# Scores before maxima in the second burst of an attention step

## The chip, the cores and the metric

The kernel runs on one core of one Trainium2 chip. The metric is device time in microseconds (us) of one execution. Before the change it was 2928.36 us, the median of 3 runs (2923.62 to 2931.43).

## The reference, cut to what matters

The input `x` has 4 sequences of 2048 tokens with 256 channels. Four blocks follow each other, each added to its input: an attention with one head of 64 (called `a` or `a0` here), a linear layer whose input is rounded to fp8, an attention with 16 heads of 16 (called `a1`), and a gated layer that mixes each token with the one before it. The change lies in the 16-head attention:

```python
Q, K, V = (proj(W_Q), proj(W_K), proj(W_V))          # 16 heads of 16
Q = _apply_rope(Q, cos, sin)
K = _apply_rope(K, cos, sin)
scores = jnp.einsum('bhsd,bhtd->bhst', Q, K) / jnp.sqrt(jnp.float32(D_K))
scores = jnp.where(causal[None, None], scores, -jnp.inf)
attn = jax.nn.softmax(scores, axis=-1)
out = jnp.einsum('bhst,bhtd->bhsd', attn, V)
```

Everything else is other work for this text: projections, transposes, the first attention, the two layers, the residual sums.

## The kernel before, in words

**Tiling.** Tokens are cut into 16 blocks of 512 (4 sequences `b`, 4 blocks `qb` in each). In the 16-head attention the heads go in 4 groups `g` of 4. A step is one `(b, qb, g, kt)`: 128 keys `kt` against the 512 queries of a block, for four heads `h` at once. A group has `4 * (qb + 1)` steps, and the program 640.

**Three shapes of the TensorE array.** A head has 16 channels, kept as a high and a low part side by side, so 32 rows are enough. The matmuls of `maxima_of` and `scores_of` therefore use tiles of 32 rows by 128 columns: head `h` uses the row group `h`, and four heads can run side by side. `weighted` (L860) multiplies the softmax weights by the values, with 128 rows by 32 columns. All other matmuls use the whole array. The text calls these three the row shape, the column shape and the full shape.

**What a step computes.** The softmax needs the maximum of each query before its exponentials. So a step does two things for two different groups:
- `scores_of(..., h)` for the present group: a matmul that adds the negated maximum (`sh`, the shift, in bfloat16, with the weights `ones`), one with the high part of the queries (`qh`) and one with the low part (`ql`), both float32r; on the diagonal two bfloat16 mask matmuls (L817) more. ScalarE then takes the exponential (`p`, L824). In the first step of a group the shift comes last.
- `maxima_of(..., h)` for the next group: a matmul with `qh` and one with `ql` (L779), both float32r, on the diagonal two mask matmuls (L788) more. VectorE then takes the maximum over the keys (`mx`, L794).

The text writes `m` for the output tile of a maximum and `s` for that of a score; each is one PSUM bank. The seven banks are shared by everything except the accumulator of `weighted`.

**The order of a step.** The kernel writes its own order out, and an order is kept on each engine by dependencies that are added at the end. A step issues

1. the first burst (L1211): scores of heads 0 and 1, maxima of heads 2 and 3,
2. `weighted` of the step before (L1217),
3. the second burst (L1229): maxima of heads 0 and 1, scores of heads 2 and 3,
4. `pull` (L1239): other work, if the planner finds it due.

`together` (L833) interleaves the four row groups of a burst: it goes round the rows and takes one matmul from each. A row that has not begun is held back while the planner counts no free bank (`room`, L827). In the first burst, a row that is through may start the scores of heads 2 and 3 early (`spare`, L853).

**The planner.** `Clock` (L41) follows each emitted instruction with assumed costs. It gives out the bank that comes free first, and `pull`, `rate_of` and `force` decide by its times in which step a piece of other work is put. In one line of it (L178) the first matmul of a row group after a change of shape is late by an amount that goes by its type and width:

```python
late = 0 if kind.endswith("float16") else 15 if mode[1] == SLOT else 45 if n <= P else 90
```

Of the kernel before, what the change touches and what calls it, by code (L numbers as in the profile page):

```python
# [30 lines left out]
HG = 4  # L31
# [159 lines left out]
def seq_kernel(  # L191
# [71 lines left out]
    order = [(b, qb) for b in range(B) for qb in range(NB)]  # L263
# [100 lines left out]
    def avbank(name):  # L364
        return pav.tile([P, BLK], F32, tag="av", name=name)

    def w2(name, dtype=F32):
        live[0] += 1
        return work.tile([P, BLK], dtype, tag="w2", name=name, bufs=W2)
# [7 lines left out]
    def done(n):  # L377
        live[0] -= n
# [418 lines left out]
    def scores_of(b, qb, g, kt, sh, pTs, h):  # L797

        r = slice(h * SLOT, (h + 1) * SLOT)
        c0 = max(kt - qb * TT, 0) * P  # L800
        keys = kT1[b, kt // TT][r, g, (kt % TT) * P : (kt % TT + 1) * P]
        diag = kt >= qb * TT
        sc = bank(f"s_{b}_{qb}_{g}_{kt}_{h}")

        q = q1[b, qb, g // 2]
        todo = [(keys, z[r, g % 2, c0:]) for z in q]
        todo.insert(0 if kt else 2, (ones[r, :], sh[r, c0:]))
        for i, (lhsT, rhs) in enumerate(todo):
            nc.tensor.matmul(  # L809
                sc[:, c0:], lhsT, rhs, start=(i == 0), stop=(i == 2 and not diag)  # L810
            )
            if i < 2 or diag:
                yield
        if diag:
            for v in range(2):
                hi = (v + 1) * P // 2
                nc.tensor.matmul(  # L817
                    sc[:, c0 : c0 + hi], mask_k[r, v, :], mask_q[r, v, :hi],
                    start=False, stop=(v == 1),
                )  # L820
                if v < 1:
                    yield
        pTs[h] = work.tile([P, BLK], F32, tag="pT", name=f"p_{b}_{qb}_{g}_{kt}_{h}", bufs=PT)
        nc.scalar.activation(pTs[h][:, c0:], sc[:, c0:], AF.Exp, scale=DK**-0.5)  # L824
        yield

    def room(h):  # L827

        clock.follow()
        now = max(clock.issue, clock.rows[h]) + 50  # L830
        return sum(b not in clock.held and t <= now for b, t in clock.banks.items())

    def together(rows, spare=()):  # L833

        rows = [[[part, False] for part in r] for r in rows]
        spare = dict(spare)
        wait = True
        while any(rows):  # L840
            moved = False
            for h, r in enumerate(rows):
                while r:
                    if wait and not r[0][1] and not room(h):
                        break
                    try:
                        next(r[0][0])
                        r[0][1] = moved = True
                        wait = True
                        break  # L850
                    except StopIteration:
                        r.pop(0)
                if not r and h in spare and any(rows) and room(h) > 3:  # L853
                    next(spare.pop(h))
            wait = moved
# [11 lines left out]
    def to_tokens(g, cs, cn, tag):  # L867

        pt = bank(f"pt_{tag}")
        for t in range(TT):  # L870
            nc.tensor.transpose(pt[:, t * P : (t + 1) * P], cs[:, t * P : (t + 1) * P], ident)  # L871
        nat = pt.rearrange("p (t h s) -> p t h s", t=TT, h=HG)
        rs = small.tile([P, TT, HG], F32, tag="rs1", name=f"rs_{tag}")
        nc.vector.reciprocal(rs, nat[:, :, :, DK])
        nc.vector.tensor_tensor(
            cn[:, :, g * HG * DK : (g + 1) * HG * DK].rearrange("p t (h d) -> p t h d", h=HG),
            nat[:, :, :, :DK],
            rs[:, :, :, None].to_broadcast([P, TT, HG, DK]),
            ALU.mult,
        )  # L880
# [133 lines left out]
    def b_of(i):  # L1014
        b, qb = order[i]
        x = xs[b, qb]
        b_load[0], q_load[0] = 14.0, 1.0
        Bq.extend([b_queries(b, qb, 0, 0), b_queries(b, qb, 0, 1), b_keys(b, qb),
                   b_project(b, qb), b_in(b, qb, x, 0), b_in(b, qb, x, 1)])
        Q.extend(b_queries(b, qb, 1, hf) for hf in range(2))  # L1020

    def end_of(i, cn):
        b, qb = order[i]
        x = xs[b, qb]
        e_load[0] = 17.0
        E.extend(end_half(b, qb, x, cn, hf) for hf in range(2))

    def begun(i):
        return all((*order[i], "cT", hf) in flags for hf in range(2))
# [66 lines left out]
    def refill(i):  # L1096

        nonlocal a_next
        if not A and a_next < min(i + (4 if not E and at[1] > 0 else 3), N):
            a_load[0] = 0.0  # L1100
            A.extend(a_of(a_next))
            a_next += 1
# [19 lines left out]
    def rate_of(i, g, kt, n):  # L1122

        to = lambda where: max(where * n - (g * n + kt), 1)
        spare = sum(loads[id(z)][0] for z in (A, Bq, Q, E)) + sum(
            a_work(*order[j]) for j in range(a_next, min(i + 4, N))
        )
        rate = min(BASE, spare / to(4))
        first = a_load[0] if a_next == i + 2 else 0.0
        if first > 0 or Bq:  # L1130
            rate = max(rate, first / to(1.5), (first + b_load[0] + e_load[0] / 2) / to(3))
        return max(rate, (q_load[0] + e_load[0]) / to(4))
# [30 lines left out]
    def due_maxima(position):  # L1163

        nonlocal b_done
        out = []
        while ahead and ahead[0][0] <= position + 1e-6:
            if ahead[0][1] > b_done:
                force(Bq)
                b_done = ahead[0][1]  # L1170
            out.append(ahead.pop()[2:])
            z = next(mq, None)
            if z:
                ahead.append(z)
        return out
# [14 lines left out]
    for G, (i, b, qb, g) in enumerate(groups):  # L1190
        n = steps[G]
        at[:] = i, g, 0, n
        if g == 0 and i + 1 < N:
            b_of(i + 1)
        av = avbank(f"av_{b}_{qb}_{g}")
        for kt in range(n):
            at[2] = kt
            count[0] += 1
            if i > 0 and (g, kt) == (0, 2):
                end_of(i - 1, cns.pop(i - 1))  # L1200
            refill(i)
            rate = rate_of(i, g, kt, n)
            credit = min(credit + rate, rate + 1.5)
            first = A if a_next == i + 2 else None
            mine = [Bq, E, Q] if i == 0 or begun(i - 1) else [E, Bq, Q]
            lists = [first] + mine if first else mine + [A]
            ms = due_maxima(G + kt / n)
            pTs, c0 = {}, max(kt - qb * TT, 0) * P
            S = [scores_of(b, qb, g, kt, shifts[G], pTs, h) for h in range(HG)]
            M = [[maxima_of(*ms[0][0], h)] if ms else [] for h in range(HG)]  # L1210
            together([[S[0]], [S[1]], M[2], M[3]], {h: S[h] for h in (2, 3) if kt})  # L1211
            if tail is not None:
                to_tokens(*tail)
                done(1)
                tail = None
            if last is not None:
                weighted(*last)  # L1217
                clock.follow()
                if narrow and clock.when(*narrow[0][4]) < clock.pe + SLACK:
                    narrow_values()  # L1220
                if last[2] != g:
                    cs = w2(f"cs_{G - 1}")
                    nc.scalar.copy(cs, last[4])
                    if g == 1:
                        while i > 0 and not begun(i - 1):
                            assert pull_first([E])
                        cns[i] = work.tile([P, TT, C], F32, tag="cn", name=f"cn_{b}_{qb}", bufs=1)
                    tail = (last[2], cs, cns[i] if g > 0 else cns[i - 1], f"c_{G - 1}")
            together([M[0], M[1], [S[2]], [S[3]]])  # L1229
            last = (b, qb, g, kt, av, pTs, c0)  # L1230
            if ms:
                ms[0][1]()
            clock.follow()
            for m in ms[1:]:
                whole_maxima(m)
            if kt == n - 1 and G + 1 < len(groups):
                shift_of(G + 1)
                clock.follow()
            pull(lists, 0.0)  # L1239
        if g == NG - 1:  # L1240
            force(E)
            force(Q)
# [84 lines left out]
```

## Time and profile before

| what | value |
|---|---|
| median of 3 runs | 2928.36 us (2923.62 to 2931.43) |
| the profiled execution's own time | 2922.84 us |
| its span, from the first to the last instruction | 2921.0 us |
| mean granted TensorE clock | 0.979 |
| TensorE (PE) busy | 2804.3 us, 96% |
| VectorE (DVE) busy | 2012.6 us, 69% |
| ScalarE (ACT) busy | 1688.2 us, 58% |
| GpSimd (POOL) busy | 1011.8 us, 35% |

A busy time is the union of the instructions' times on that engine. Matmuls are pipelined and run side by side in the row shape, so a busy TensorE is not one at its peak, and a matmul that stands in the array behind another one of its row group counts as busy. `PEld` is TensorE's loading of weights. Lines such as L779 are lines of the kernel.

### The profile page before, as it was taken

To read this page: it belongs to the slowest core of one execution; us is meant where nothing else is said; L and a number is where in the kernel's file an instruction comes from. 1 tells how busy PE (TensorE), PEld (TensorE's weight loads), DVE (VectorE), ACT (ScalarE), POOL (GpSimd) and SP (SyncE) were. 2 spreads that over 40 slices of the span, in tenths; PEclk is the share of its full clock that TensorE was granted. 3 is DMA by queue.
4 is the path that set the end of the run, shared out by engine and by line. 5 is a ranking of instruction groups with operands and counts; after the bars stand their busy time and mean duration, and the time that the engine had idled before them with its cause. 6 is when DMAs were issued, how large, how long until landed. Compare 5 with 4: busy or idle time off the path is not lost.

```text
span 2921.0 us, 68258 instructions
## 1 busy us (share of the span) xinstructions
PE 2804.3 (96%) x27616; PEld 1580.6 (54%) x27616; DVE 2012.6 (69%) x4279; ACT 1688.2 (58%) x3553; POOL 1011.8 (35%) x1534
## 2 busy tenths in 40 slices
PE   6899999999999999999999999999999999999997
PEld 3555555555456555555556555555545655555443
DVE  4567667787556786787746777778764677678761
ACT  2456555566665556656665555656566565665663
POOL 4534425242333514514215342523323342450001
PEclk8799999999999999999999999999999999999999
DMA  3000000000000000000000000000000000000000
GB/s 91 1 12 5 12 12 16 12 2 26 2 12 16 5 23 2 16 12 5 23 12 5 12 5 23 5 23 1 27 2 12 16 5 16 1 9 1 5 1 12
DMA packets 28781, 36.70 MB, mean 13 GB/s; under 512 B 3312, under 2 KB 22064, under 8 KB 28464
## 3 DMA queue, kind: packets, MB, share of 16 engines
q1 hardware_dynamic: 28464, 32.32, 3.9%
q8 instruction: 217, 3.56, 0.5%
q14 instruction: 100, 0.82, 0.1%
HBM read 11.24 MB, written 8.39 MB: 7 GB/s over the span
## 4 chain that ended last, share of the span: by engine, by line
PE 79%; DVE 11%; POOL 5%; issue 3%; ACT 1%; DMA 0%; SPq 0%; POOLq 0%; ACTq 0%; DVEq 0%
PE av L860 18%; PE s L809 16%; PE m L779 14%; DVE mx L794 7%; PE pq_a L421 3%; PE pv_a L421 2%; PE av_a L578 2%; PE m_a L524 2%; PE po_f L421 2%; PE pk_f L928 2%; PE pw_f L421 2%; PE pr_f L421 2%; PE m L788 1%; PE s_a L548 1%; PE pt_c L871 1%
## 5 line engine op out<-in xcount | busy, mean ns | idle before, releaser
L794 DVE TENSOR_REDUCE mx<-m 128x1 f32<-128x512 f32 (+3 forms) x2560 | 1405.1, 603 | 531.6 <-PE m L779 237.6
L824 ACT ACTIVATE p<-s 128x512 f32<-128x512 f32 (+3 forms) x2560 | 1214.2, 534 | 814.3 <-PE s L809 445.8
L779 PE MATMUL m<-kT_a,qh_a 32*128 32x512 f32 (+3 forms) x2560 | 686.1, 458 | 13.7 <-ACT p L824 4.0
L809 PE MATMUL s<-qh_a,kT_a 32*128 32x512 f32 (+3 forms) x2560 | 672.6, 508 | 0.5 <-ACT p L824 0.5
L860 PE MATMUL av<-p,v_a 128*32 128x512 f32 (+3 forms) x5120 | 641.0, 545 | 0.1
L779 PEld LDWEIGHTS m<-kT_a,qh_a 32*128 32x128 f32 x2560 | 296.0, 184 | 493.9 <-issue 161.1
L779 PE MATMUL m<-kT_a,ql_a 32*128 32x512 f32 (+3 forms) x2560 | 559.3, 368 | 0.0
L809 PE MATMUL s<-ql_a,kT_a 32*128 32x512 f32 (+3 forms) x2560 | 494.3, 365 | 0.0
L809 PE MATMUL s<-sh,ones 32*128 32x512 bf16 (+3 forms) x2560 | 481.0, 355 | 3.1 <-DVE mx L794 2.3
L779 PEld LDWEIGHTS m<-kT_a,ql_a 32*128 32x128 f32 x2560 | 297.0, 188 | 3.3 <-issue 1.0
L809 PEld LDWEIGHTS s<-qh_a,kT_a 32*128 32x128 f32 x2560 | 259.7, 189 | 35.3 <-issue 23.7
L809 PEld LDWEIGHTS s<-ql_a,kT_a 32*128 32x128 f32 x2560 | 257.3, 187 | 2.8 <-issue 0.2
L809 PEld LDWEIGHTS <-ones 32*128 32x128 bf16 x2560 | 128.7, 91 | 171.4 <-issue 150.5
L860 PEld LDWEIGHTS av<-p,v_a 128*32 128x32 f32 x5120 | 112.4, 108 | 161.8 <-issue 118.7
L443 POOL CAST pad<-nm 128x16 bf16<-128x16 f32 x64 | 17.0, 266 | 380.9 <-DVE nm L989 352.3
L590 POOL TENSOR_TENSOR sum_a<-sum_a,p_a 128x512 f32<-128x512 f32 (+1 forms) x128 | 146.3, 1143 | 5.0
L788 PE MATMUL m<-mask_k,mask_q 32*128 32x64 bf16 x2048 | 147.0, 196 | 0.0
L817 PE MATMUL s<-mask_q,mask_k 32*128 32x64 bf16 (+1 forms) x2048 | 140.4, 207 | 0.0
L590 POOL TENSOR_TENSOR cx_a<-cx_a,avs_a 128x512 f32<-128x512 f32 (+1 forms) x64 | 73.1, 1143 | 155.1 <-ACT avs_a L588 155.1
L421 PE MATMUL pq_a<-wqkv,xT_a 128*128 128x512 f32 x256 | 122.8, 602 | 1.6 <-DVE mx L794 1.3
L950 POOL TENSOR_TENSOR x<-x,sg_f 128x512 f32<-128x512 f32 x32 | 41.4, 1294 | 177.3 <-DVE sg_f L949 177.1
L935 POOL TENSOR_TENSOR ka_f<-ka_f 128x512 f32<-128x512 f32 x32 | 33.2, 1038 | 186.1 <-ACT ka_f L934 186.1
(164 smaller groups left out, 4015.6 us busy)
## 6 DMA issues: line engine op xcount, KB each, us to landing
x<-in_x SPq DMA_DIRECT2D x16, 512.0 KB, 4.0
out_y<-x SPq DMA_DIRECT2D x32, 256.0 KB, 2.1
qh_a<-th_a SPq DMA_DIRECT2D x32, 128.0 KB, 2.3
ql_a<-tl_a SPq DMA_DIRECT2D x32, 128.0 KB, 2.3
kT_a<-th_a SPq DMA_DIRECT2D x16, 128.0 KB, 2.3
kT_a<-tl_a SPq DMA_DIRECT2D x16, 128.0 KB, 2.3
wqkv<-in_wqkv1T SPq DMA_DIRECT2D x1, 768.0 KB, 7.3
wc<-in_wfT SPq DMA_DIRECT2D x1, 256.0 KB, 5.7
```

The source lines that it names most:

```text
L421: nc.tensor.matmul(dst, lhsT[:, k, t * P : (t + 1) * P], w[:, k, :], start=(k == 0), stop=(k == CK - 1),)
L524: nc.tensor.matmul(sc[:, :w], q[:, t * P : (t + 1) * P], kT0[kb][:, :w], start=(q is qh), stop=(kb < qb and q is ql),)
L578: nc.tensor.matmul(av[z * SLOT : (z + 1) * SLOT, c0:], v0[kt // TT][:, kt % TT + j, d * SLOT : (d + 1) * SLOT], pTs[j][:, c0:], start=True ...
L590: nc.gpsimd.tensor_tensor(to[:, c0:], to[:, c0:], add[:, c0:], ALU.add)
L779: nc.tensor.matmul(sc[:, :w], q1[b, qb, g // 2][i][r, g % 2, t * P : (t + 1) * P], kT1[b, kb][r, g, :w], start=(i == 0), stop=(kb < qb and ...
L788: nc.tensor.matmul(sc[:, w - P + lo : w - P // 2 + lo], mask_q[r, v, :], mask_k[r, v, lo : lo + P // 2], start=False, stop=(v == 1),)
L794: nc.vector.reduce_max(mx[:, t, h, kb : kb + 1], sc[:, :w], axis=AX.X)
L809: nc.tensor.matmul(sc[:, c0:], lhsT, rhs, start=(i == 0), stop=(i == 2 and not diag))
L817: nc.tensor.matmul(sc[:, c0 : c0 + hi], mask_k[r, v, :], mask_q[r, v, :hi], start=False, stop=(v == 1),)
L824: nc.scalar.activation(pTs[h][:, c0:], sc[:, c0:], AF.Exp, scale=DK**-0.5)
L860: nc.tensor.matmul(av[h * SLOT : (h + 1) * SLOT, c0:], v1[b, kt // TT][:, kt % TT, at : at + SLOT], pTs[h][:, c0:], start=(kt == 0), stop= ...
L928: nc.tensor.matmul(pk[:, d * HALF : (d + 1) * HALF], wk[:, k, d * P : (d + 1) * P], xk[:, k, :], start=(k == 0), stop=(k == CK - 1),)
```

## The change

The second burst goes round its rows in the order 2, 3, 0, 1 in place of 0, 1, 2, 3. Rows 2 and 3 hold the scores of heads 2 and 3, rows 0 and 1 the maxima of heads 0 and 1. The first burst and all other callers keep the order 0, 1, 2, 3. No instruction is added or removed.

```diff
-    def together(rows, spare=()):
+    def together(rows, spare=(), order=range(HG)):
...
-            for h, r in enumerate(rows):
+            for h in order:
+                r = rows[h]
                 while r:
                     if wait and not r[0][1] and not room(h):
                         break
...
-            together([M[0], M[1], [S[2]], [S[3]]])
+            together([M[0], M[1], [S[2]], [S[3]]], order=(2, 3, 0, 1))
```

## The prediction

> **What bounds the kernel now.** I read the page first: the span, the engines' busy times and the chain that ended last.
>
> ```profile
> span 2921.0 us, 68258 instructions
> PE 2804.3 (96%) x27616; PEld 1580.6 (54%) x27616; DVE 2012.6 (69%) x4279; ACT 1688.2 (58%) x3553; POOL 1011.8 (35%) x1534
> PE 79%; DVE 11%; POOL 5%; issue 3%; ACT 1%; DMA 0%; SPq 0%; POOLq 0%; ACTq 0%; DVEq 0%
> PE av L860 18%; PE s L809 16%; PE m L779 14%; DVE mx L794 7%; PE pq_a L421 3%; PE pv_a L421 2%; PE av_a L578 2%; PE m_a L524 2%; PE po_f L421 2%; PE pk_f L928 2%; PE pw_f L421 2%; PE pr_f L421 2%; PE m L788 1%; PE s_a L548 1%; PE pt_c L871 1%
> ```
>
> TensorE sets the time, and the three groups that the change moves around lead the chain. But 7% of it (some 200 us) is VectorE's maximum, so there are places where TensorE waits for a bank. Next, the timeline of one second burst, behind `weighted` and ahead of other work:
>
> ```profile
> 2705.62 0.61 PE L860 MATMUL av<-p,v_a 128*32 128x512 f32 x4
> 2706.16 0.50 PE L779 MATMUL m<-kT_a,qh_a 32*128 32x512 f32 x2
> 2706.17 0.39 PE L809 MATMUL s<-sh,ones 32*128 32x512 bf16 x2
> 2706.21 0.58 PE L809 MATMUL s<-qh_a,kT_a 32*128 32x512 f32 x2
> 2706.49 0.40 PE L779 MATMUL m<-kT_a,ql_a 32*128 32x512 f32 x2
> 2706.62 0.40 PE L809 MATMUL s<-ql_a,kT_a 32*128 32x512 f32 x2
> 2706.92 1.29 DVE L794 TENSOR_REDUCE mx<-m 128x1 f32<-128x512 f32 x2 [0.68 <-PE m L779]
> ```
>
> All four rows start within 0.02 us. A maximum's second matmul comes 0.33 us behind its first; the scores' third comes 0.46 us behind the shift, and ends the burst. Now a first burst that begins with the shift after another shape, which is the order that the change gives to the second burst:
>
> ```profile
> 242.61 0.39 PE L809 MATMUL s<-sh,ones 32*128 32x512 bf16 x2
> 242.62 0.50 PE L779 MATMUL m<-kT_a,qh_a 32*128 32x512 f32 x2
> 242.65 0.58 PE L809 MATMUL s<-qh_a,kT_a 32*128 32x512 f32 x2
> 242.96 0.39 PE L779 MATMUL m<-kT_a,ql_a 32*128 32x512 f32 x2
> 243.07 0.40 PE L809 MATMUL s<-ql_a,kT_a 32*128 32x512 f32 x2
> ```
>
> The same distances: 0.34 us for the maximum, 0.46 us for the scores. Last, the chain of waits in a stretch of steps with no other work between the bursts:
>
> ```profile
> 2689.57 1.01 PE av L860 x8
> 2690.57 0.33 PE m L779
> 2690.90 0.24 PE s L809 x3
> 2691.14 0.14 PE m L779 x2
> 2691.28 0.69 DVE mx L794
> 2691.97 0.04 issue
> 2692.01 0.73 PE m L779 x2
> ```
>
> Such a step is bare: its second burst and the next step's first burst want eight banks, there are seven, and the eighth tile waits until VectorE has taken the first maximum.
>
> **The change part by part.** I read TensorE's matmul records one by one against the order of the built program, before and after.
>
> *What moves.* 488 second bursts began with two maxima and two shifts behind a column-shape matmul; now 483 begin with shifts. 57 bursts that hold scores alone do not change. No DMA moves, no engine gets an instruction more, and ScalarE's and VectorE's own order within a burst stays.
>
> *The start after the change of shape.* Second bursts begin 70 ns ahead of the modelled end of the last matmul when a maximum leads (425 records), 67 ns when a shift leads (57). So a shift in front costs 3 ns. Stalls there are absent: 9 of 10 lie within 1 ns of that.
>
> *The loading of weights.* The groups by line give 184 ns for a maximum's weights and 91 ns for the shift's. Were the load exposed, 93 ns in 483 bursts would be 45 us gained; the 70 against 67 ns say that it is hidden, and I take nothing. The Trainium skill ("TensorE: Matmul & The Clock Gate", section "LDWEIGHTS (loading the stationary operand)") has a load's time depend on its columns alone, which would make the two equal and the gain zero as well; the rows differ by half, and only the start times settle it.
>
> *The dear first matmul.* At 512 columns a float32r matmul takes 213 ns when it follows another in its row group, and 336 ns when it is the first there after a change of shape. That is 120 ns for rows 0 and 1 in every second burst, 59 us in all, if a shift in front of the burst paid it for all rows. In 188 second bursts with a maximum in front the distance is 336 ns; in 58 first bursts behind L421 with the shift in front, 337. The price belongs to each row group, and the change leaves each row its own first matmul. Value: nothing.
>
> *The order of issue.* In 302 first bursts the rows start at 0, 3, 4 and 7 ns (shift, shift, maximum, maximum); in second bursts now at 0, 3, 9 and 13 (maxima, shifts). With the 3 ns above, scores come 6 ns earlier and maxima 7 ns later. Where a burst of the same make-up stands alone between other shapes, its length can be compared: 715 ns shift first (117 bursts) against 726 ns maximum first (114) at 512 columns, 647 against 661 with scores of 384, but 673 against 667 with scores of 256, where the maximum's row is the longer. Some 280 lone bursts at -10 ns, 75 at +6 and some 190 bare ones at +7 (the maximum's bank ends their loop): -2.8 + 0.5 + 1.3 = -1.0 us. Bounds: -11 and +7 ns on all, -6 to +4 us. The Trainium skill (same page, "Part 3: Packing small matmuls — row/col tiling", "The mechanism") has matmuls start strictly in program order. By that rule the scores' `qh`, which is issued behind the maximum's `ql`, could not start before it, and the new order would free it 0.28 us earlier, over 100 us for 483 bursts. The burst at 2706 shows `qh` at 2706.21 and `ql` at 2706.49: the rows run on their own, and I go by the row.
>
> *Rows that the planner holds back.* Where it counts fewer than four free banks, the last row of the round begins late. Before, that was a score in 35 bursts; after, a maximum in 39, and in 13 of these both maxima (52 tiles). A lone burst with a late row took 1102 against 726 ns when it was a score, and 941 against 715 when the first burst's last row was late: 39 x 0.226 - 35 x 0.376 = -4 us. But 34 of the 52 tiles (11 first and 23 second maxima) stand in bare steps, where a late maximum can hold the loop, up to 34 x 0.376 = +13 us. I take +1, nearer to the first, since the first of the two maxima, whose bank ends the loop, is late in only 11.
>
> *The other work.* This is where most of the change lies. The planner's times move by some ns, and it decides anew: of 1248 pieces of other work on TensorE, 624 land in another step, most within five steps. Their number is the same, but stretches of row-shape matmuls fall from 1097 to 1084, and 13 fewer stretches of full-shape work begin. I price each kind by its mean time in the trace, from the end of the matmul before to the start of the one behind. Stretches with one step's share of maxima and scores: 23 fewer at 0.796 us, -18.3. Stretches of two bursts: 12 more at 2.09, +25.2. Two more of four bursts with other work behind at 3.62, +7.2; two fewer with three pairs of maxima at 2.14, -4.3; three fewer with scores in both and maxima in one at 1.13, -3.4; the rest (scores alone) +1.5. Sum +7.9 us. Joining two stretches of other work saves 0.07 us of the change of shape and some 0.06 to 0.11 us of a first matmul: 13 x 0.15 = -2. That leaves +6 us. A bare step hides less than two covered ones, so fewer interruptions do not pay. The spread of such stretches around their mean is some 0.3 us, half of them change, and three of the four sequences repeat one pattern, so that errors add up: I take +-9 us.
>
> **Sum.** -1 + 1 + 6 = +6 us on the profiled execution's 2922.84, that is 2928.8. The median of the runs lies 5.5 us above that execution; carried over, 2928.4 + 6 = 2934.4, which I call 2934. A measurement of this kernel tells about 0.3%, 9 us, from no change.
>
> **The rivals.**
>
> *Slower: late maxima in the bare loop.* Place: the bare steps, some 190 stretches. Mechanism: a maximum's bank is freed only when its last matmul is through and VectorE has taken 0.69 us over it; behind two scores in the issue order it may come through when they do. VectorE already waits for scores to release it (the list of waits has 141 us, 147 times, on L809). Price: the scores' last matmul ends 0.14 us behind the maximum's in the burst at 2706 (2706.62 + 0.40 against 2706.49 + 0.39); 190 x 0.14 = +27 us, with the +6 some 2961. It decides once the second matmul of full maxima stands behind the scores' last in the program. In the built order that is so for 13 first maxima and 39 second ones, and for none before; of the remaining full ones none. So it acts in a tenth of the places unless late rows delay their successors too. A mild form, +15 us in all, is the likelier.
>
> *Faster: less switching.* 26 fewer changes of shape and scores that reach ScalarE earlier. If the new places of the other work happen to fill bare steps that are dearer than the mean (two bursts and more cost 2.1 to 3.6 us), ten such at 0.9 us of stall (2.09 less five matmuls of 213 ns in a row group and 120 for the first) and the 2 us of switching give -11, some 2917.
>
> *Faster: the shift pays for all rows.* 120 ns in 483 bursts, less where scores end the burst anyway; at most -58, some 2870. The 58 first bursts speak against it.
>
> *It does nothing* cannot be: the built order differs in every second burst.
>
> **How the numbers follow.** The forecast, +6 with +-9, has 0.62: 0.38 within 0.3%, 0.21 slower, 0.03 faster. Late maxima 0.22, all slower. Less switching 0.12, of which 0.01 stays within. The shift that pays for all 0.04. Faster 0.18, same 0.39, slower 0.43. Range: from 2917, the less-switching case, to 2960, nearly the full late-maxima case. The likeliest case alone has 2925 to 2943.
>
> **What would show it.** Right: in second bursts the shift at 0 and the maximum 4 ns behind it; 0.33 us between a maximum's two matmuls as before; L779, L809 and L860 within a few us of their busy times; VectorE's part of the chain a little larger. Wrong: a distance near 0.22 us between a maximum's matmuls (the first rows' price is gone), or VectorE's L794 at 9% or more of the chain (late maxima).

## The result, and the profile after

The changed kernel takes 2969.97 us (median of 4 runs, 2956.06 to 2979.46) against 2928.52 us for the kernel before, measured beside it: a ratio of 1.0139 [1.0094, 1.0185]. The forecast was 2934 with a range up to 2960, so the time lies above the range. Of all the executions behind the ratios in this text one is left out, of `warm_waits_before` below: it took 3862 us at a granted clock of 0.613. The profiled execution took 2965.06 us. Here is its page: the span, the busy times and the chain that ended last.

```profile
span 2963.1 us, 68203 instructions
PE 2832.6 (96%) x27616; PEld 1593.1 (54%) x27616; DVE 2022.1 (68%) x4279; ACT 1684.3 (57%) x3553; POOL 1014.3 (34%) x1534
PE 77%; DVE 13%; POOL 6%; issue 2%; ACT 2%; DMA 1%; SPq 0%; POOLq 0%; DVEq 0%; ACTq 0%
PE s L809 18%; PE av L861 17%; PE m L779 11%; DVE mx L794 8%; PE pq_a L421 3%; PE av_a L578 2%; PE pv_a L421 2%; PE pk_f L929 2%; PE po_f L421 2%; PE m_a L524 2%; PE pr_f L421 2%; PE pw_f L421 2%; PE pt_c L872 1%; PE s_a L548 1%; PE m L788 1%
```

TensorE's busy time grew by 28.3 us with the same 27616 matmuls, and VectorE's part of the chain from 11% to 13%. No new line appears in the chain. The group of the maxima's first matmuls (L779, `qh`) went from 686.1 to 711.6 us busy, the second (`ql`) from 559.3 to 580.4; their mean durations went from 458 to 465 ns and from 368 to 372 ns.

One second burst in the timeline of the changed kernel (start, length in us, the instruction). It has the same make-up as the one shown in the prediction:

```profile
2747.61 1.07 PE L861 MATMUL av<-p,v_a 128*32 128x512 f32 x8
2748.61 0.39 PE L809 MATMUL s<-sh,ones 32*128 32x512 bf16 x2
2748.61 0.50 PE L779 MATMUL m<-kT_a,qh_a 32*128 32x512 f32 x2
2748.65 0.58 PE L809 MATMUL s<-qh_a,kT_a 32*128 32x512 f32 x2
2748.95 0.40 PE L779 MATMUL m<-kT_a,ql_a 32*128 32x512 f32 x2
2749.07 0.40 PE L809 MATMUL s<-ql_a,kT_a 32*128 32x512 f32 x2
```

The shift now leads. A maximum's two matmuls are 0.34 us apart (2748.61 to 2748.95) and the scores' third comes 0.46 us behind the shift, as the prediction had both. The chain of waits in a bare step:

```profile
2741.34 1.00 PE av L861 x8
2742.33 0.32 PE s L809 x2
2742.65 0.12 PE m L779 x2
2742.77 0.12 PE s L809 x2
2742.89 0.16 PE m L779 x2
2743.05 0.69 DVE mx L794
2743.78 0.73 PE m L779 x2
```

From `weighted` to the maximum that had to wait for its bank it takes 2.44 us (2741.34 to 2743.78), and before it took the same (2689.57 to 2692.01). The bursts themselves do not hold the 42 us by which the span grew.

What did change is the clock. The mean granted TensorE clock was 0.979 before and is 0.966 now, and in the records it has two values, 1.00 and 0.50. Adding up the stretches at 0.50 within the span gives 125.5 us before and 200.6 us after, 75.1 us more. A stretch at half speed can cost at most half of its length, and it costs that only if matmuls fill all of it; that would be 37.6 of the 42.1 us by which the span grew. The experiments below put the price lower, at some 0.35 us for each microsecond at half speed, which makes it 26 us. The other 16 us or so are lost at full speed: TensorE's idle time (span less busy time) rose from 116.7 to 130.5 us. In the four runs of the changed kernel the clock was 0.969, 0.966, 0.961 and 0.960 at 2956, 2965, 2975 and 2979 us, so from run to run the time moves with the clock as well.

### The profile page after: what moved, and what is told of

Same layout as the page of the kernel before. It is cut to its first block, busy times and chain, and to the rows that moved or that the text cites. A ratio compares the mean times of both kernels' runs of the same rounds, so it can differ in the third digit from the quotient of the medians.

```text
span 2963.1 us, 68203 instructions
## 1 busy us (share of the span) xinstructions
PE 2832.6 (96%) x27616; PEld 1593.1 (54%) x27616; DVE 2022.1 (68%) x4279; ACT 1684.3 (57%) x3553; POOL 1014.3 (34%) x1534
## 4 chain that ended last, share of the span: by engine, by line
PE 77%; DVE 13%; POOL 6%; issue 2%; ACT 2%; DMA 1%; SPq 0%; POOLq 0%; DVEq 0%; ACTq 0%
PE s L809 18%; PE av L861 17%; PE m L779 11%; DVE mx L794 8%; PE pq_a L421 3%; PE av_a L578 2%; PE pv_a L421 2%; PE pk_f L929 2%; PE po_f L421 2%; PE m_a L524 2%; PE pr_f L421 2%; PE pw_f L421 2%; PE pt_c L872 1%; PE s_a L548 1%; PE m L788 1%
## 5 line engine op out<-in xcount | busy, mean ns | idle before, releaser
L794 DVE TENSOR_REDUCE mx<-m 128x1 f32<-128x512 f32 (+3 forms) x2560 | 1402.8, 602 | 546.2 <-PE m L779 245.2
L779 PE MATMUL m<-kT_a,qh_a 32*128 32x512 f32 (+3 forms) x2560 | 711.6, 465 | 17.2 <-DVE mx L794 5.8
L779 PE MATMUL m<-kT_a,ql_a 32*128 32x512 f32 (+3 forms) x2560 | 580.4, 372 | 0.0
L779 PEld LDWEIGHTS m<-kT_a,qh_a 32*128 32x128 f32 x2560 | 309.8, 187 | 94.7 <-DVE mx L794 53.5
L779 PEld LDWEIGHTS m<-kT_a,ql_a 32*128 32x128 f32 x2560 | 311.7, 191 | 1.5
L443 POOL CAST pad<-nm 128x16 bf16<-128x16 f32 x64 | 17.4, 273 | 438.5 <-DVE nm L990 421.4
L421 PE MATMUL pq_a<-wqkv,xT_a 128*128 128x512 f32 x256 | 122.7, 601 | 2.0 <-ACT p L824 2.0
L713 DVE TENSOR_TENSOR rb_a<-qk_a,rb_a 128x256 fp32r<-128x256 f32 x64 | 40.6, 634 | 82.5 <-ACT rb_a L712 82.2
```

The costliest lines, as they stand in the source:

```text
L421: nc.tensor.matmul(dst, lhsT[:, k, t * P : (t + 1) * P], w[:, k, :], start=(k == 0), stop=(k == CK - 1),)
L779: nc.tensor.matmul(sc[:, :w], q1[b, qb, g // 2][i][r, g % 2, t * P : (t + 1) * P], kT1[b, kb][r, g, :w], start=(i == 0), stop=(kb < qb and ...
L794: nc.vector.reduce_max(mx[:, t, h, kb : kb + 1], sc[:, :w], axis=AX.X)
```

## The experiments

Three theories were to be told apart.
- **The order itself:** late maxima, a bank that comes free later, or the held-back rows cost the time.
- **The places of other work:** the planner decided anew, and the new places cost far more than the 6 us that the prediction gave them.
- **The clock as a consequence:** TensorE runs slower because it waits more for other reasons, and the half-speed stretches add nothing of their own. Its opposite is that the half-speed stretches are the cost.

### The order alone, and the places alone

The planner's comparisons of times (in `pull`, `pull_first`, `narrow` and `ripe`) are replaced by a list of answers, taken from the build of the other kernel. `order_only` has the new order with the answers of the kernel before, so that every piece of other work stands in the step where it stood before. `places_only` has the old order with the changed kernel's answers.

```diff
-                    if t is None or t > clock.pe + SLACK:
+                    if decide(t is None or t > clock.pe + SLACK):
...
-                if t is not None and (best is None or t < best[0] - SLACK):
+                if decide(t is not None and (best is None or t < best[0] - SLACK)):
...
+def DECIDE(places, now):
+    return next(places)
```

> The second burst goes round its rows 2, 3, 0, 1, but every piece of other work stands in the step where the kernel before has it (the planner's answers are replayed). Theory A (the new places of the other work cost the time): as before, ratio 0.997 to 1.003, some 2928 us, half-speed time of TensorE as before (about 80 us behind the start). Rival B (the order itself costs, by late maxima or by less TensorE activity per window): ratio 1.010 or more, some 2965 us, half-speed time about 150 us. Theory C (time is lost through the granted clock, whatever displaces it): in each of these runs the time less half of the half-speed time is the same within 6 us.

> The second burst keeps the order 0, 1, 2, 3, but every piece of other work stands in the step where the changed kernel has it. Theory A: ratio 1.010 to 1.018, some 2970 us. Rival B: ratio 0.997 to 1.003. If both parts count, each shows a part and the two ratios multiply to about 1.014.

Measured: `order_only` 2935.14 us, 1.0027 [1.0017, 1.0036]. `places_only` 2977.56 us, 1.0169 [1.0149, 1.0188]. So the order of issue costs some 8 us, and the places alone cost some 49 us, all of the loss. The two do not add up exactly: with both, the ratio is 1.0139, its interval overlapping that of the places alone. The clocks of the profiled executions follow: 0.976 with 138.6 us at half speed, and 0.962 with 224.3 us.

The spans can be split with an estimate that is worked out further down (0.35 of the half-speed time is lost to the clock):

| kernel | span, us | at half speed, us | span less 0.35 of that, us |
|---|---|---|---|
| before | 2921.0 | 125.5 | 2877.1 |
| changed | 2963.1 | 200.6 | 2892.9 |
| `order_only` | 2932.4 | 138.6 | 2883.9 |
| `places_only` | 2977.5 | 224.3 | 2899.0 |

So the clock takes more than half of what the changed kernel and `places_only` lose (26 of 42 us, 35 of 56), and some 16 to 22 us are lost besides.

### Where the clock drops

Behind the first 145 us (a start in which it changes often in both kernels), the clock drops 13 times before and 23 times after, not counting one at the very end. In `places_only` it drops 25 times. These drops lie at one kind of place: 12 of 13, 21 of 23 and 24 of 25 begin in the last four steps of a group or directly behind them; such steps are 256 of the 640. There the maxima of the next group end. VectorE forms `nm`, GpSimd splits it into three bfloat16 parts with four operations (L443 to L446), and only then can TensorE turn the result into the shift rows (the transposes into `pt_sh`, L453) and go on. The scores are narrow there, since the diagonal leaves few columns. One such end, that of the last group of the second block in the third sequence, in the timeline before:

```profile
1763.11 1.13 PE L484 MATMUL pq_a<-xT_a,wqk 128*128 128x256 f32 x4
1764.08 1.00 PE L421 MATMUL pv_a<-wv,xT_a 128*128 128x64 f32 x8
...
1766.37 0.26 PE L817 MATMUL s<-mask_q,mask_k 32*128 32x64 bf16 x4
1766.56 0.40 PE L453 MATMUL pt_sh<-ident_b,pad 128*128 128x128 bf16 x4
```

and after:

```profile
1789.37 0.96 PE L861 MATMUL av<-p,v_a 128*32 128x256 f32 x8
...
1790.56 0.26 PE L817 MATMUL s<-mask_q,mask_k 32*128 32x64 bf16 x4
1792.22 0.40 PE L453 MATMUL pt_sh<-ident_b,pad 128*128 128x128 bf16 x4 [1.41 <-POOL pad L446]
```

GpSimd's part of it, after:

```profile
1790.94 0.25 POOL L443 CAST pad<-nm 128x16 bf16<-128x16 f32 x1 [15.53 <-DVE nm L990]
1791.27 0.23 POOL L444 TENSOR_TENSOR rest<-nm,pad 128x16 f32<-128x16 f32 x1
1791.57 0.25 POOL L445 CAST pad<-rest 128x16 bf16<-128x16 f32 x1
1791.90 0.27 POOL L446 TENSOR_TENSOR pad<-rest,pad 128x16 bf16<-128x16 f32 x1
```

Before, two pieces of other work (L484 and L421, some 1.9 us) stood in the last steps and covered the 1.23 us that GpSimd takes. The planner put them elsewhere, and TensorE waits 1.41 us, as the bracket says. The stretches around this end show what follows. The columns are the stretch, the busy time of five engines, the granted clock, the share of DMA and GB/s. Before:

```profile
1763.20:1766.60 3.40, 3.40 (x41) 2.67 (x42) 2.17 (x5) 1.58 (x5) 1.01 (x4) 1.00 0.61 195
1766.60:1776.80 10.20, 10.03 (x93) 6.28 (x92) 8.22 (x18) 4.84 (x11) 0.00 (x0) 1.00 0.28 65
```

after:

```profile
1789.70:1793.10 3.40, 2.00 (x30) 1.08 (x24) 1.66 (x5) 1.18 (x5) 1.85 (x6) 0.99 0.00 0
1793.10:1803.30 10.20, 10.20 (x79) 6.13 (x76) 6.05 (x12) 3.88 (x8) 0.02 (x1) 0.50 0.01 2
```

In the 3.4 us around the wait TensorE is busy for 2.00 us, and then it has the clock of 0.50 for 10.2 us. The wait costs 1.41 us; what the half speed behind it costs is measured further down, some 3.5 us.

The list of TensorE's waits has no such sum by itself (line waited for, total us, times, longest). Before:

```profile
PE pt_sh L453 <- POOL pad L446: 26.1, 32, 2.5
```

after:

```profile
PE pt_sh L453 <- POOL pad L446: 30.1, 32, 2.5
```

Only 4 us more. What counts is which of these waits are long. Three of the four sequences repeat the pattern: at the end of group 3 of the second block the wait goes from 0 to 1.41 us, at that of group 1 from 0 to 0.73.

How full the array is can be worked out for each window of 3.4 us: the columns of the matmuls recorded in it, each weighted by the share of rows and columns that it uses, over what a full array takes in at 512 columns in 213 ns. In the windows ahead of a drop this use was at most 0.31 before and 0.34 after; 95% of the full-speed windows without a drop behind them have 0.34 or more. The use alone does not decide, though: of some 750 windows without a drop, 14 before and 27 after lie below those highest values. This is a description of where the drops lie, not yet a proof of their cause.

### Is the clock the cause? Work added for nothing

If the clock is the cause, pointless work in the waits should make the kernel faster. Ahead of the transposes into `pt_sh`, four matmuls of a full array with 512 columns write the same bank, and the transposes overwrite it. The planner does not see them, so all other work stays where it is. `warm_after` and `warm_before` do so at all 64 group ends, in the changed kernel and in the one before.

```diff
+    warm = const.tile([P, BLK], BF16, name="warm")
+    nc.gpsimd.memset(warm, 1.0)
...
     def shift_rows(pad, sh, name):
         pt = bank(f"pt_{name}")
+        if name.startswith("sh_a") is False:
+            for _ in range(4):
+                nc.tensor.matmul(pt, ident_b, warm, start=True, stop=True)
+            clock.seen = len(nc.cur_bb.bb.instructions)
         for t in range(TT):
```

> The changed kernel, with four more bfloat16 matmuls of 512 columns over the whole array ahead of the transposes of each group's shift (64 places), whose results are overwritten. TensorE waits there for GpSimd, 30 us in all in the profile. The work added is 64 x 4 x 0.213 = 55 us at full clock. Theory C: they keep windows from falling below the activity that the gate asks, so that the half-speed time falls from 160 us by a third or more (some 25 us of time), while no more than 25 us of the added work lies outside the waits: ratio to before 1.005 to 1.014, mean granted clock above 0.970. Rival D (the low clock is a consequence of the waits and costs nothing itself, since TensorE waits anyway): ratio 1.02 or more, clock no matter.

> The same four matmuls per group in the kernel before. TensorE's wait there is 26 us in all, and the half-speed time 80 us behind the start, of which about a third follows a group's end. Theory C: the half-speed time falls by 20 to 40 us, worth 10 to 20 us, against up to 29 us of added work outside the waits: ratio 0.998 to 1.008. Rival D: ratio 1.010 to 1.015.

Measured: `warm_after` 2960.35 us, 1.0109 [1.0094, 1.0124], and `warm_before` 2939.95 us, 1.0034 [1.0019, 1.0048]. Some 55 us of added matmuls (64 x 4 x 213 ns) cost the changed kernel nothing, and the kernel before only 11 us. The time at half speed fell from 200.6 to 89.8 us and from 125.5 to 80.7 us. At 0.35 the clock gave back an estimated 39 and 16 us, and part of the work lay in waits. That the changed kernel became faster can't be read from this pair alone, as the intervals of 1.0109 and 1.0139 overlap.

Most of these matmuls stand where TensorE had no wait. The last pair puts them only where it had one: `warm_waits_after` at the 21 group ends where the changed kernel's profile has a wait of 0.68 us or more, `warm_waits_before` at the 13 ends where the kernel before has 0.8 us or more.

```diff
+WARM = ('sh_0_0_1', 'sh_0_1_0', 'sh_0_1_2', ...)
...
-        if name.startswith("sh_a") is False:
+        if name in WARM:
```

> The changed kernel with the four extra matmuls only at those 21 group ends where its own profile shows TensorE waiting 0.68 us or more for the shift (22.9 us of waits; the work added is 21 x 4 x 0.213 = 17.9 us). Theory C (the granted clock): nearly all of it lies in waits, and the windows at these ends no longer fall below the gate's level. About 9 of the 23 drops to half speed followed these ends; at 6.9 us of half speed each that is 31 us: ratio to before 1.002 to 1.008, clock 0.972 or more. Rival D (the waits cost, the clock does not): time as in the changed kernel, 1.012 to 1.016, since the waits themselves stay.

> The kernel before with the same four matmuls at the 13 group ends where its profile shows a wait of 0.8 us or more (14.5 us of waits; 11.1 us of work added). Theory C: about 5 of its 13 drops follow these ends, at 6 us of half speed each, 15 us: ratio 0.993 to 0.999. Rival D: 0.999 to 1.003.

Measured: `warm_waits_after` 2937.07 us, 1.0026 [1.0017, 1.0034]. With 17.9 us of work more, the changed kernel is 33 us faster. Its half-speed time is 125.4 us, as before the change (125.5), with 10 drops in place of 23. The same group end as above, in its timeline (L453 is L460 here):

```profile
1768.91 0.26 PE L824 MATMUL s<-mask_q,mask_k 32*128 32x64 bf16 x4
1769.10 1.04 PE L457 MATMUL pt_sh<-warm,ident_b 128*128 128x512 bf16 x3
1770.57 0.40 PE L460 MATMUL pt_sh<-ident_b,pad 128*128 128x128 bf16 x4 [0.43 <-POOL pad L449]
```

and its stretches:

```profile
1766.50:1769.90 3.40, 3.35 (x49) 2.06 (x48) 3.20 (x8) 1.45 (x6) 0.48 (x2) 1.00 0.03 5
1769.90:1780.10 10.20, 9.67 (x100) 5.06 (x98) 7.86 (x18) 6.16 (x12) 2.09 (x5) 1.00 0.00 0
```

The transposes still cannot begin before GpSimd is through; three of the four matmuls are in the record, and a wait of 0.43 us is left. But the clock stays at 1.00, and 100 matmuls run in the next 10.2 us where 79 did.

The two pages agree with this. The first two lines of this kernel's:

```profile
span 2935.3 us, 68351 instructions
PE 2823.1 (96%) x27678; PEld 1586.5 (54%) x27700; DVE 2022.5 (69%) x4279; ACT 1683.0 (57%) x3553; POOL 1014.5 (35%) x1535
```

TensorE's idle time falls from 130.5 to 112.2 us, about the 17.9 us of work added, and its busy time falls too, by 9.5 us, although it does more.

Since all other work stands in the same steps, the two traces can also be compared piece by piece. Cut into 64 stretches of ten steps (from the end of one exponential to the end of another), 45 have the same half-speed time in both kernels. Together these 45 differ by 0.6 us, although eight of the group ends with added matmuls lie in them. In the other 19 the half-speed time is 75.3 us less and the length 28.4 us less, which is all of the difference between the spans (27.8 us). The stretch that holds the group end shown above goes from 52.36 to 48.81 us, with its 10.2 us at half speed gone. So the half-speed stretches are a cost and not only a consequence: the wait for the pads is as long as ever, only its length without work is not, and the added matmuls change the time where they change the clock and nowhere else. This is also the price used above: 28.4 over 75.3 is 0.38 us for each microsecond at half speed, 0.34 without the first ten steps; 0.35 is an estimate from these two.

`warm_waits_before` measured 2926.24 us, 0.9981 [0.997, 0.9992]: a version that beats both kernels, by less than the 0.3% named in the prediction. That its gain comes from the clock is not shown. Its profiled execution has 128.3 us at half speed against 125.5 before; the mean clock over its runs is 0.979 against 0.977.

### Is it these places, or any new places?

Four kernels keep the old order and change a constant of the planner, so that other work lands elsewhere. `jig120` alters the assumed cost of a change of shape (L174), by which 156 of 640 steps get other work than before; `base180` and `base170` the rate at which other work is handed out (370 and 381 steps); `end3x12` raises that rate by a quarter in the last three steps of a group and lowers it by 5% elsewhere (410 steps).

```diff
-            now = max(now, self.pe, t) + 110
+            now = max(now, self.pe, t) + 120
```

> The kernel before with one of the planner's assumed costs altered: 120 in place of 110 for a change of shape. The order of the bursts is the old one; other work changes in 156 of the 640 steps. The built order has 193.9 us of other work (columns at 2.4 GHz) in the last three steps of the 64 groups, against 213.1 before and 191.3 in the changed kernel. Theory F (these steps are narrow and wait for each other; other work in them keeps TensorE's activity up, so less of it means more half-speed time): half-speed time 170 to 210 us, ratio 1.008 to 1.013. Rival G (any new place costs, because the planner's constants were fitted to the old ones; how much goes by the number of moved steps): some 1.007, as 156 of 338 moved steps. Rival H (the places don't matter by themselves): 0.998 to 1.003.

```diff
-    BASE = 1.75
+    BASE = 1.80
```

> The kernel before with the planner's rate of other work set to 1.80 in place of 1.75. Other work changes in 370 steps; 200.9 us of it stand in the last three steps of the groups. Theory F: half-speed time 150 to 190 us, ratio 1.004 to 1.010. Rival G: 1.014 or more, as in the changed kernel with its 338 moved steps. Rival H: 0.998 to 1.003.

with 1.70 in place of 1.80:

> The same rate at 1.70. Other work changes in 381 steps; 220.7 us of it stand in the last three steps of the groups, more than before. Theory F: half-speed time 90 to 125 us, ratio 0.993 to 1.000. Rival G: 1.014 or more. Rival H: 0.998 to 1.003.

```diff
             rate = rate_of(i, g, kt, n)
+            rate *= 1.25 if kt >= n - 3 else 0.95
```

> The kernel before, with the planner's rate multiplied by 1.25 in the last three steps of a group and by 0.95 in the others. Other work changes in 410 steps; 228.1 us of it stand in the last three steps of the groups, but 144 steps have none at all (138 before, 144 in the changed kernel). Theory F: half-speed time 60 to 110 us, ratio 0.987 to 0.998. Rival G: 1.015 or more. Rival I (steps without any other work decide, wherever they are): 1.012 to 1.016, as in the changed kernel.

| kernel | ratio | half speed, us | drops | span less 0.35 of the half speed, us | other work in the last three steps, us |
|---|---|---|---|---|---|
| before | 1 | 125.5 | 13 | 2877.1 | 213.1 |
| changed | 1.0139 [1.0094, 1.0185] | 200.6 | 23 | 2892.9 | 191.3 |
| `jig120` | 1.0117 [1.0095, 1.0139] | 191.7 | 27 | 2897.3 | 193.9 |
| `base180` | 1.0228 [1.0205, 1.025] | 274.0 | 26 | 2905.7 | 200.9 |
| `base170` | 1.014 [1.0111, 1.017] | 158.9 | 11 | 2908.8 | 220.7 |
| `end3x12` | 1.0103 [1.0082, 1.0124] | 156.2 | 19 | 2900.8 | 228.1 |

The last column is an estimate from the columns of each piece of work. A theory rested on it: that the more other work stands at the ends, the better. It fell. `base170` and `end3x12` have more of it than the kernel before, and both are slower by 1% or more. They lose less to the clock than the changed kernel, and instead some 24 to 32 us at full speed, where I have not followed them. `jig120` came out as that theory had it, `base180` lost more than twice what it allowed. The rival that the loss goes by the number of moved steps fell as well: 156 moved steps cost 1.17%, and 410 cost 1.03%. In `end3x12` the wait for the pads even rose, to 38.4 us. That any other places cost something held in all five kernels that were re-placed, from 1.0 to 2.3%. So the places before are better than those that five small shifts of the planner's times or rates led to. What makes them good as a whole stays open; shown is only that in the changed kernel some covers of group ends are gone, and that giving these ends matmuls again takes back most of the loss (33 of 41 us).

## Why the prediction was wrong, point by point

**The start, the weights, the dear first matmul.** These held. `order_only` has all of them at once and is 1.0027 [1.0017, 1.0036]. With the price of a first matmul paid by the shift for all rows, it would have been up to 58 us faster; the 0.34 us between a maximum's matmuls show that each row still pays. The rule cited there that matmuls start strictly in program order would have given over 100 us and is out for the row groups here; a load of weights that was not hidden would have given 45, and is out too.

**The order of issue and the held-back rows.** The sum was 0 (-1 and +1), with bounds of -6 to +4 and up to +13 for late rows. Measured by `order_only`: 0.27% or 8 us, between 5 and 10. The size is off, but within the bounds of the two together, and as far as the runs tell it is clock. Over the runs (10 against 14, each with its span and its granted clock) the span is 7.3 us longer and some 24 us more lie at half speed, which at 0.35 is 8 us. For the order itself nothing is left that could be told from the 0 of the sum. Why the order alone lowers the clock stays open. Late maxima as a rival mechanism of 15 to 27 us (the burst at 2706 gives 0.13 us in place of 0.14, with the 0.40 us that its line shows, so 25) are refuted: VectorE's L794 has 6% of the chain in `order_only` against 7% before. In the changed kernel it has 8%, short of the 9% that I had set as the sign; the growth comes with the places and not with the order, as `places_only` has 8% as well.

**The other work: the step that failed.** The prediction said rightly that most of the change lies here, and counted 624 of 1248 pieces moved. Then it priced each kind of stretch by its mean duration and took +6 with a spread of 9. `places_only` measured +49 us, five times that spread. Two things went wrong in it. The first is a term that it left out, and so put at nothing: the clock. `places_only` has 98.8 us more at half speed, some 35 of the 56.5 us by which its span is longer. The second is the term itself: the other 22 us stand where the prediction had +6 with +-9. How far this second part is off depends on the price; at the upper bound of one half it would be 7 us and the clock 49. A mean duration takes the clock of the kernel before as given and cannot tell that a stretch without other work, at one place, slows the 3.4 to 20.5 us behind it. The sign for this was in the page of the kernel before. A granted clock of 0.979 meant 125.5 us at half speed, some 44 us lost at 0.35, in places that could be found, and that a change which moves other work could open more of them.

**The spread.** It was taken from durations of stretches. The five re-placed kernels show what the spread of this planner is: 1.0 to 2.3%, and none of them went towards faster. The spread of 9 us reached only to 0.5%.

**The signs.** Both signs that I had named for being wrong (0.22 us between a maximum's matmuls, 9% for L794) stayed out, while the time was wrong. Of the signs for being right, the busy times "within a few us" failed for L779 by 25.5 and 21 us. The clock is only a part of it. `order_only` has 14.3 and 11.5 us more with mean durations of 459 and 369 ns, 1 ns longer than before, so that there these matmuls overlap less and are hardly longer. With the new places they are longer, too: 465 and 372 ns in the changed kernel, 469 and 376 in `places_only`.

**Less switching** has no support: the places alone cost time.

## What to carry to other kernels

Where a planner places work by assumed times, an edit that moves these times by nanoseconds is two edits; build each alone, by replaying one build's decisions with the other's order, before the durations of either are argued about. Look at where the clock drops, not only at its mean: a wait of a microsecond among narrow matmuls can cost several microseconds behind it. If such a wait cannot be covered by useful work, a few matmuls into a bank that is overwritten anyway can be cheaper than the wait, though only where there is a wait: at all ends they cost 0.34% in the kernel before, at the 13 with a wait they gained 0.19%.

## What the runs showed of the hardware

- **The clock can halve after a short wait.** A window of 3.4 us in which TensorE was busy for 2.00 us, with one wait of 1.41 us, was followed by 10.2 us at a clock of 0.50. Of the 21 group ends of the changed kernel with a wait of 0.68 us or more, 11 had a drop at its end or within 3.4 us behind it, so the wait alone does not decide. Behind the start and ahead of the very end, half-speed stretches came in lengths of 3.4, 6.8, 10.2 and 13.7 us (17.1 once in `base180`, 20.5 once there and once in `places_only`), that is, within rounding, in multiples of 3.4. The Trainium skill ("TensorE: Matmul & The Clock Gate", section "What's actually happening") has windows of about 3.4 us and two rates as well, but lets the lower rate follow an idle window; by its rule in "Why this matters for your kernels", no idle gaps above some 3 us, the wait shown here would cost its own 1.41 us and no more. The row differs, and the measurement decides. The same page's section on "psum-queue depth-cycling" is nearer to it: there, frequent short idle times are enough.
- **Half speed costs less than half of its time.** It cost 0.34 to 0.38 us for each microsecond between two kernels that differ in the added matmuls alone (75.3 us less at half speed, 28.4 us shorter).
- **The clock moves with the time from run to run.** The changed kernel's four runs differ by 0.8% (2956 to 2979 us), the four of the kernel before beside them by 0.3% (23 others by 0.5%). That a kernel with more windows near the point of the drop repeats less well would fit, but was not tried.
- **Pointless work can be free.** 55 us of full-array matmuls at the group ends left the changed kernel's time no longer (1.0109 against 1.0139, overlapping intervals), since the clock gave back some 39 us (an estimate, at 0.35) and part of them lay in waits.
